# A two-layer state-space kernel on one core: layer 0's preparation for the second batch moved beside the first batch's forward scans

## The chip, the core and the metric

The kernel runs on one core of a Trainium2 chip. The metric is the device time of one execution in microseconds (us); the time of a version is the median of its runs. TensorE is called PE, VectorE DVE, ScalarE ACT, GpSimd POOL; SP is the queue that issues most DMAs. Everything is fp32.

## The reference, cut to what matters

The input x is 2 batches of 256 channels over 4096 positions. Layer 0 is a selective state-space model on the group-normed input, added to x. Layer 1 is the same model with 512 inner channels, run once forward and once with time reversed over the layer-normed result, and then eight experts of three matrix products each, mixed by a router whose features are a mean over both batches.

```python
# layer 0: group norm, then
xs, z = jnp.split(seq @ W_in, 2, axis=-1)
xc = _silu(conv_b + sum(xp[:, k:k + L, :] * conv_w[:, k] for k in range(d_conv)))
dbc = xc @ W_x
dt = softplus(dbc[..., :dt_rank] @ W_dt + b_dt)          # then Bm, Cm from dbc
h = h * exp(dt * A) + (dt * x) * B                       # per time step, 16 states
y = sum_s(h * C) + xc * D
out = (y * _silu(z)) @ W_out
# layer 1: the same with its own weights on _ln(t), forward and flipped: y_fwd + y_bwd + x
# experts on _ln(t):
feat = jnp.mean(x, axis=0); w = softmax(feat @ Wr + br)
h = relu(bn(x @ W1 + b1)); h = relu(bn(h @ W2 + b2)); y = h @ Wo + bo    # for 8 experts
out = sum_e(y[e] * w[e])
```

## The kernel before, in words

Six jobs run one after the other (`jobs`): job 0 is layer 0 of batch 0 (the first), job 1 layer 1 forward of batch 0, job 2 layer 1 backward of batch 0, and jobs 3, 4 and 5 the same of batch 1. Each job goes through 8 chunks of 512 positions. A layer-0 job has nj = 2 tiles of 128 inner channels, a layer-1 job nj = 4.

The work of a chunk is cut in quads: 32 channels by 4 states on the partitions, 4 groups of 32 channels along the free axis. Eight quads make two channel tiles. A quad has two halves, and a half is a slot, the unit of order in the whole program: 1280 slots, 16 per layer-0 chunk and 32 per layer-1 chunk. In a slot ACT makes exp(dt A) of the next slot in PSUM (`emit_decay`, L664, with the small joins L675 and the carried state L709), DVE runs one scan of 1024 steps (L690), and either DVE multiplies the states by C (L699, 760 half quads) or POOL does it for a whole or half quad (L715). POOL makes dt x times B of each quad (L654). PE sums the states into y (L723) after a first product with diag(D) (`emit_skip`, L730), whose matrix ACT builds anew for each tile of each chunk (`emit_diagonal`, L735). DVE multiplies by the gate (L742), and `finish` projects out (L761), adds x and stores.

Before its scans a chunk is prepared (`prepare`): input product xs (L414), a convolution as small matmuls (L452), its SiLU on DVE (L466, xc), the product to B, C and dt's low-rank part (L481), dt by softplus (three ACT ops, DVE L513), dt x on POOL (L517, xdt), and the gate sz (L543). dt and dt x go to DRAM and come back replicated over the states (`load_rep`, 1 MB each), B and C likewise (`load_states`). Ahead of that stands the norm: for layer 0 a scaling on ACT (L341) with group statistics, for layer 1 forward a layer norm in several steps (`norm`); backward reads back what forward stored.

The order is written out by hand. `Slots` keeps, for each slot and queue, a list of functions; `SLOTS` says at which slot before the chunk's first one each step of the preparation is issued (a product of PE in one slot, the ACT step in the next, the DVE step after that), and the main loop runs a slot's queues in the order sp, pe, sums, pe2, act, dve, pool. Each engine then works strictly in its issued order, and waits where data or a buffer isn't there. PSUM gives the preparation three banks in rotation, tanh and softplus share three buffers (`th`). The activation table is switched twice a chunk (L569), to the set with ln for the softplus and back.

`experts` plans expert work into the scan phase: from the moment a chunk's features are ready (the backward job of its batch), two halves of three layers per expert go to slots where PE (3.8 products a slot), ACT and PSUM have room by counts that every step reports (`sl.count`). They use buffers of their own: weights ew0, ew1, ew2, input en, hidden eh1 and eh2, output eu. What is finished goes to DRAM (`u_dram`). What doesn't fit by the last slot is computed in the tail, after the scans: `pairs` goes chunk by chunk and expert by expert, 24 passes of PE each (L1208, L1227), and between two of them a share of the side work of that chunk: load x, add the bias, load and add what was computed early (`add_early`, L1177 to L1179, two DVE ops each), and the router of the next chunk (`routes`). The order of chunks is by how many of their experts were computed early, fewest first. In the kernel before 81 of the 128 are early: all of batch 0's 64, and batch 1's chunks 7 and 6 with one of chunk 5.

The statistics for batch 1's group norm are made in job 2 (`chunk_stats`, L998; `group_norm`), eight loads of x with two DVE ops each.

## Time and profile before

| | us |
|---|---|
| median of 3 runs | 5111.3 |
| lowest and highest run | 5107.4, 5111.66 |
| span of the profiled execution (its only time) | 5111.0 |
| start, to the first scan | 60.0 |
| job 0, 128 slots | 466.3 |
| job 1, 256 slots | 872.5 |
| job 2, 256 slots | 882.6 |
| job 3, 128 slots | 467.5 |
| job 4, 256 slots | 876.2 |
| job 5, 256 slots | 869.9 |
| after the last scan | 616.0 |

| busy over the span | us | share |
|---|---|---|
| PE matmul | 4272.0 | 84% |
| DVE | 4580.6 | 90% |
| ACT | 3682.0 | 72% |
| POOL | 4409.1 | 86% |

The parts by job run from the start of a job's first scan to the start of the next one's. A share over the whole span hides that the parts have different limits; busy time by part is to be read with it. Idle time on an engine is charged to what ended it. A matmul's end is modelled, so a busy PE isn't PE at its peak.

### The profile page before, as it was taken

What the parts mean: (1) busy time and instruction counts of PE and PEld (TensorE: products, weight loads), DVE (VectorE), ACT (ScalarE), POOL (GpSimd) and SP (SyncE); (2) the same over time, 40 slices, a digit from 0 to 9 for tenths busy, and PEclk for the clock granted to TensorE, in tenths of its full rate; (3) what the DMA queues carried; (4) which work ended last, traced back from release to release, by engine and by line L of the source; (5) the groups of instructions that cost most, each with busy time, mean ns of one, the idle gap of its engine ahead of it and who ended that gap; (6) DMA issues with size and microseconds to landing.
All of it is one profiled execution on the core that took longest, in us unless ns stands there. A gap on an engine that the chain in (4) does not pass through costs nothing. (4 is left out here: it accounts for less than half of the span.)

```text
span 5111.0 us, 47355 instructions
## 1 busy us (share of the span) xinstructions
PE 4272.0 (84%) x14920; PEld 1474.5 (29%) x14920; DVE 4580.6 (90%) x3089; ACT 3682.0 (72%) x7476; POOL 4409.1 (86%) x1442
## 2 busy tenths in 40 slices
PE   5777767776668988988888889999999999988999
PEld 1222222221212332333322233333333333333444
DVE  6998999999999999999989999999999999936633
ACT  5777677777767888888887888888878888832232
POOL 5998999999999999999989999999999999921110
PEclk8778888888878999999999999999999999999999
DMA  5454433344444454556655545455555544555522
GB/s 179 149 176 160 165 137 125 136 136 149 156 141 155 170 177 170 187 171 201 209 182 180 181 166 200 165 179 173 181 179 181 169 166 160 175 188 181 193 103 87
DMA packets 322604, 847.85 MB, mean 166 GB/s; under 512 B 35816, under 2 KB 108016, under 8 KB 280368
## 3 DMA queue, kind: packets, MB, share of 16 engines
q1 hardware_dynamic: 318064, 817.43, 46.7%
q0 software_dynamic: 4288, 27.40, 1.4%
q8 instruction: 118, 1.93, 0.2%
q14 instruction: 134, 1.10, 0.1%
HBM read 656.88 MB, written 187.83 MB: 165 GB/s over the span
## 5 line engine op out<-in xcount | busy, mean ns | idle before, releaser
L654 POOL TENSOR_TENSOR bq<-rxdt,bc 128x2048 f32<-128x2048 f32 x640 | 2892.9, 4542 | 24.5 <-issue 13.2
L664 ACT ACTIVATE da<-rdt,w_a 128x512 f32<-128x512 f32 x2560 | 1757.0, 686 | 97.2 <-DVE bq L690 51.7
L690 DVE TENSOR_TENSOR_SCAN da<-da,h_state,bq 128x1024 f32<-128x1024 f32 x664 | 1559.1, 2348 | 44.9 <-ACT da L664 26.2
L715 POOL TENSOR_TENSOR bq<-bq,bc 128x2048 f32<-128x2048 f32 (+1 forms) x280 | 1179.8, 4214 | 22.5
L690 DVE TENSOR_TENSOR_SCAN bq<-da,h_state,bq 128x1024 f32<-128x1024 f32 x456 | 1058.6, 2338 | 20.7 <-ACT da L664 20.6
L723 PE MATMUL y<-bq,stack 128*32 128x512 f32 x5120 | 758.9, 681 | 315.1 <-POOL bq L715 294.0
L699 DVE TENSOR_TENSOR bq<-da,bc 128x1024 f32<-128x1024 f32 x760 | 926.5, 1219 | 16.0
L912 PE MATMUL e<-eh,ew 128*128 128x512 f32 x1296 | 631.1, 617 | 54.0 <-ACT eh L923 13.9
L709 ACT COPY h_state<-da 128x2 f32<-128x2 f32 x759 | 118.9, 157 | 617.7 <-DVE bq L699 615.4
L675 ACT ACTIVATE bq<-h_state,bq,a 128x1 f32<-128x1 f32 x1120 | 430.3, 384 | 0.6
L723 PEld LDWEIGHTS y<-bq,stack 128*32 128x32 f32 x5120 | 143.0, 118 | 878.6 <-POOL bq L715 416.5
L912 PEld LDWEIGHTS e<-eh,ew 128*128 128x128 f32 x1296 | 231.6, 192 | 445.4 <-issue 221.4
L1212 ACT ACTIVATE h<-hp,of,sc 128x512 f32<-128x512 f32 x188 | 145.9, 777 | 290.8 <-PE hp L1208 272.7
L452 PE MATMUL conv<-xs,w_conv 64*64 64x512 f32 x2560 | 332.1, 608 | 21.7 <-ACT xs L436 17.8
L414 PE MATMUL z<-nx,w_in 128*128 128x512 f32 x640 | 324.9, 639 | 26.5 <-DVE sp L513 12.0
L414 PE MATMUL xs<-nx,w_in 128*128 128x512 f32 x640 | 316.6, 624 | 23.4 <-DVE xc L466 8.4
L912 PE MATMUL e<-en,ew 128*128 128x512 f32 x648 | 308.4, 605 | 28.3 <-DVE fcen L809 15.7
L761 PE MATMUL o<-sz,w_out 128*128 128x512 f32 x640 | 306.3, 619 | 0.0
L923 ACT ACTIVATE eh<-e,of,sc 128x512 f32<-128x512 f32 x324 | 245.6, 769 | 30.6 <-PE e L912 30.2
L517 POOL TENSOR_TENSOR xdt<-sp,xc 128x512 f32<-128x512 f32 x160 | 203.4, 1275 | 49.7 <-DVE sp L513 49.7
L730 PE MATMUL y<-xc,w_d 128*128 128x512 f32 x320 | 193.5, 689 | 56.5 <-DVE sz L742 56.3
L690 DVE TENSOR_TENSOR_SCAN da<-da,bq 128x1024 f32<-128x1024 f32 x96 | 219.5, 2287 | 5.3 <-issue 2.5
(139 smaller groups left out, 4914.3 us busy)
## 6 DMA issues: line engine op xcount, KB each, us to landing
rxdt<-xdtd SPq DMA_DIRECT2D x160, 1024.0 KB, 6.8
rdt<-dtd SPq DMA_DIRECT2D x160, 1024.0 KB, 6.6
bc<-bcd SPq DMA_DIRECT2D x384, 256.0 KB, 3.3
ew<-in_W SPq DMA_DIRECT2D x162, 256.0 KB, 4.4
u<-u SPq DMA_DIRECT2D x81, 512.0 KB, 4.3
dtd<-sp SPq DMA_DIRECT2D x160, 256.0 KB, 3.5
xdtd<-xdt SPq DMA_DIRECT2D x160, 256.0 KB, 3.8
u<-eu SPq DMA_DIRECT2D x77, 512.0 KB, 6.7
```

What stands on the lines that cost most here:

```text
L414: nc.tensor.matmul(ps, job.w["in", half][:, k, j * P : (j + 1) * P], rhs, start=(k == 0), stop=(k == KC - 1),)
L452: nc.tensor.matmul(v[r][64 * col : 64 * col + 64, :], job.w["conv"][rows, 2 * jp + j, k, :], ck["xs", jp][rows, j, k : k + T] if k < 4 els ...
L654: nc.gpsimd.tensor_tensor(bq[g], ck["rxdt", j], over_groups(ck["bc", 0, sg]), ALU.mult)
L664: nc.scalar.activation(da[g, h][:, k, :], cks[i]["rdt", j][:, q, :], AF.Exp, scale=steps[i][0].w["a"][:, j, q * SG + sg : q * SG + sg + 1],)
L675: nc.scalar.activation(bq[g][:, q, 0:1], job.h[:, j, sg, q : q + 1], AF.Identity, scale=cks[i]["a0", j][:, h, sg : sg + 1], bias=bq[g][:, ...
L690: nc.vector.tensor_tensor_scan(b if on_pool(g, h) else d, d, b, job.h[:, j, sg, 2 * h : 2 * h + 1] if c else 0.0, ALU.mult, ALU.add,)
L699: nc.vector.tensor_tensor(bq[g][:, two, :], d, cks[i]["bc", 1, sg].rearrange("p (o t) -> p o t", o=1).to_broadcast([P, 2, T]), ALU.mult,)
L715: nc.gpsimd.tensor_tensor(b, b, cks[i]["bc", 1, sg].rearrange("p (o t) -> p o t", o=1).to_broadcast([P, groups, T]), ALU.mult,)
L723: nc.tensor.matmul(y[i, j][q * CG : (q + 1) * CG, :], stack, bq[g][:, q, :], start=False, stop=(sg == SG - 1),)
L761: nc.tensor.matmul(v[m], job.w["out"][:, j, m * P : (m + 1) * P], ck["sz", j], start=False, stop=(j == job.nj - 1),)
L912: nc.tensor.matmul(ps, ew[l][:, k, m * P : (m + 1) * P], key[x][:, k, :], start=(k == 0), stop=(k == KC - 1),)
L923: nc.scalar.activation(key[dst][:, m, :], key["ps", l, m], AF.Relu, bias=of[:, l, e, m : m + 1], scale=sc[:, l, e, m : m + 1],)
```

## The change

The preparation of job 3 (layer 0 of batch 1) no longer stands before each of its chunks. Chunk c of it is issued within the slots of chunk c + 1 of job 1 (for c = 7, the first chunk of job 2), at the slots of `AHEAD_SLOTS` from that chunk's first one. Its input x and its xc take turns in eh1, the scaled input is in en, sz in eu; xc, sz, dt, dt x and B, C go to DRAM tensors of their own, and job 3 loads xc and sz back tile by tile (16 loads each). The counts for the planner go to the slots where the steps now are.

Layer 0's large weights (W_in, convolution, W_x, W_dt) are loaded once, in the experts' buffers ew0, ew1, eh2 and ew2, and serve both layer-0 jobs; layer 1's keep their own. W_dt is loaded into both halves of the partitions, since job 3's B, C, dt rows take partitions 64 to 127 of the tile that job 1 uses.

Batch 1's statistics move to job 0 (a load every 14 slots, in eu), its group norm to 11 slots before job 1. Around it, job 1's own steps move by one or a few slots (`late`, `xs`, `log`), and the ln table is chosen earlier there, so that both softplus run under one choice. Job 3 switches no tables of its own.

D's diagonals are built once a job, in one buffer for all its tiles, two slots before the tile's first use (slot 8j - 2). The averaging matrix of the layer norms is a column read with a zero step; the group norm's matrix is rebuilt at each of its two uses.

In the built program this makes 86 early experts instead of 81 (batch 1's chunk 5 has six, not one), 20 diagonals instead of 160, 98 table loads instead of 116, and 1862 entries in SP's order instead of 1793.

```diff
+AHEAD = 3
+AHEAD_SLOTS = dict(x=-7, scale=-5, xs=(-1, 0), conv=(2,), dbc=10, dt=(14, 22), z=(-4, 12))
+NARROW_W = {"w_in0": "ew0", "w_in1": "ew1", "w_conv": "eh2"}
...
-    mean_w = const.tile([P, P], F32, name="mean_w")
-    nc.vector.memset(mean_w, 1.0 / C)
...
+    columns = const.tile([P, 6], F32, name="columns")
+    one_col, eps3, eps5, eps10, huge, mean_col = (columns[:, k : k + 1] for k in range(6))
+    for column, value in (
+        (one_col, 1.0), (eps3, 1e-3), (eps5, 1e-5), (eps10, 1e-10), (huge, HUGE), (mean_col, 1.0 / C),
+    ):
         nc.vector.memset(column, value)
+    mean_w = mean_col.to_broadcast([P, P])
...
+        dbc_rows = const.tile([P, T], F32, name="dbc_rows")
...
         def load_weights(job, tag, s0):
             nj, w = job.nj, {}
             job.w = w
+            job.matrices = jobs[0].w if job is jobs[AHEAD] else w
+
+            def weight(key, home, shape, name):
+                if job.layer:
+                    w[key] = wp.tile(shape, F32, tag=home, name=f"{name}_{tag}")
+                elif key == "dt":
+                    w[key] = w["x_dt"][:, nj * XC : nj * XC + shape[1]]
+                elif key == "x":
+                    w["x_dt"] = wk.tile([P, KC * C], F32, tag="ew2", name=f"{name}_{tag}")
+                    w[key] = w["x_dt"][:, : nj * XC].rearrange("p (j n) -> p j n", j=nj)
+                else:
+                    w[key] = wk.tile(shape, F32, tag=NARROW_W[home], name=f"{name}_{tag}")
...
-                nc.sync.dma_start(w["dt"], job.params["W_dt"])
+                weight("dt", "w_dt", [XC, job.din], "w_dt")
+                for rows in range(0, P if job.layer == 0 else XC, XC):
+                    nc.sync.dma_start(w["dt"][rows : rows + XC, :], job.params["W_dt"])
...
+            def halve():
                 nc.scalar.mul(w["conv"][:, :, 4, :], w["conv"][:, :, 4, :], 0.5)
...
+            def diagonal(j):
+                if j == 0:
+                    job.diagonal = wp.tile([P, nj, P], F32, tag="w_d", name=f"w_d_{tag}")
+                nc.scalar.mul(
+                    job.diagonal[:, j, :].rearrange("p (q c) -> p q c", q=SG),
+                    ident.rearrange("p (c q) -> p q c", q=SG), w["vec"][:, j, V_D : V_D + 1],
+                )
+
+            for j in range(nj):
+                sl.put(s0 + 8 * j - 2, "act", lambda j=j: diagonal(j))
             sl.put(s0 - 39, "sp", load_small)
+            sl.put(s0 - 31, "act", small)
+            sl.put(s0 + 19, "sp", load_out)
+            if job is jobs[AHEAD]:
+                return
...
-            sl.put(s0 - 31, "act", small)
+            sl.put(s0 - 31, "act", halve)
...
+            if job is not jobs[AHEAD]:
+                keep(job, "kept", tag)
...
+            g16 = wk.tile([P, T], F32, tag="th", name=f"g16_{tag}", bufs=3)
+            g16, blk8 = g16[:, : P // 8], g16[:, P : 2 * P]
+            nc.vector.tensor_reduce(g16, ident.rearrange("p (g k) -> p g k", k=8), AX.X, ALU.add)
+            nc.vector.tensor_scalar(
+                blk8.rearrange("p (g k) -> p g k", k=8),
+                g16.rearrange("p (g o) -> p g o", o=1).to_broadcast([P, P // 8, 8]),
+                1.0 / 8, None, ALU.mult,
+            )
...
+            if job is jobs[AHEAD]:
+                return
...
+            late = 1 if NCH < i < 2 * NCH else 0
             for d, queue, fn in (
                 (-48, "sp", load_x), (-44, "pe", mean), (-43, "dve", centre), (-42, "act", square),
-                (-41, "pe", variance), (-40, "act", roots), (-39, "dve", divide), (-39, "pool", add),
+                (late - 41, "pe", variance), (late - 40, "act", roots), (late - 39, "dve", divide), (late - 39, "pool", add),
                 (-35 if c else -38, "act", affine), (-34, "sp", store),
...
+            if NCH < i <= 2 * NCH + 1:
+                at = dict(at, xs=(-31, -29, -24, -23), log=-18)
+            ahead = job is jobs[AHEAD]
+            at_rows = slice(XC, 2 * XC) if ahead else slice(0, XC)
+
+            def of_chunk(key, j, bufs, home):
+                if not ahead:
+                    ck[key, j] = wk.tile([P, T], F32, tag=key, name=f"{key}_{tag}_{j}", bufs=bufs)
+                else:
+                    if j == 0:
+                        ck[key] = wk.tile([P, KC, T], F32, tag=home, name=f"{key}_{tag}")
+                    ck[key, j] = ck[key][:, j, :]
+                return ck[key, j]
+
+            def stored(key):
+                ck[key, "d"] = drp.tile([P, KC, T], F32, name=f"{key}d_{tag}")
+                nc.sync.dma_start(ck[key, "d"], ck[key])
+
+            def loaded(key, j, bufs):
+                ck[key, j] = wk.tile([P, T], F32, tag=key, name=f"{key}_{tag}_{j}", bufs=bufs)
+                nc.sync.dma_start(ck[key, j], ck[key, "d"][:, j, :])
+
+            def scaled():
+                ck["nx"] = wk.tile([P, KC, T], F32, tag="en", name=f"nx_{tag}")
+                for k in range(KC):
+                    nc.scalar.activation(
+                        ck["nx"][:, k, :], ck["x"][:, k, :], AF.Identity,
+                        bias=job.gb[:, k : k + 1], scale=job.gs[:, k : k + 1],
+                    )
...
+            def load_x():
+                ck["x"] = wk.tile([P, KC, T], F32, tag="eh1", name=f"x_{tag}")
+                nc.sync.dma_start(
+                    ck["x"], a["x"][job.batch].rearrange("(k p) l -> p k l", p=P)[:, :, job.cols(c)]
+                )
...
-                    ck["xc", j] = wk.tile([P, T], F32, tag="xc", name=f"xc_{tag}_{j}", bufs=6)
                     nc.vector.scalar_tensor_tensor(
-                        ck["xc", j], th[r], 1.0, v[r], ALU.add, ALU.mult
+                        of_chunk("xc", j, 6, "eh1"), th[r], 1.0, v[r], ALU.add, ALU.mult
...
-                    ck["dbc"] = wk.tile([XC, T], F32, tag="dbc", name=f"dbc_{tag}")
-                    nc.scalar.activation(ck["dbc"], v["ps"][:XC], AF.Identity, bias=one_row[:XC])
-                    ck["bc"] = bcd.tile([2, NS, T], F32, tag="bc", name=f"bcd_{tag}")
+                    ck["dbc"] = dbc_rows[at_rows, :]
+                    nc.scalar.activation(ck["dbc"], v["ps"][at_rows, :], AF.Identity, bias=one_row[at_rows])
+                    ck["bc"] = (
+                        drp.tile([2, NS, T], F32, name=f"bcd_{tag}") if ahead
+                        else bcd.tile([2, NS, T], F32, tag="bc", name=f"bcd_{tag}")
+                    )
...
-                        v["ps"], job.w["dt"][:, j * P : (j + 1) * P], ck["dbc"], start=True, stop=True
+                        v["ps"], job.matrices["dt"][at_rows, j * P : (j + 1) * P], ck["dbc"], start=True, stop=True
...
                 def store(key):
-                    d = ck["rep", key, j] = bcd.tile(
-                        [P, T], F32, tag=f"{key}{j}", name=f"{key}d_{tag}_{j}"
+                    d = ck["rep", key, j] = (
+                        drp.tile([P, T], F32, name=f"{key}d_{tag}_{j}") if ahead
+                        else bcd.tile([P, T], F32, tag=f"{key}{j}", name=f"{key}d_{tag}_{j}")
...
-                    ck["sz", j] = wk.tile([P, T], F32, tag="sz", name=f"sz_{tag}_{j}", bufs=8)
                     nc.vector.scalar_tensor_tensor(
-                        ck["sz", j], v["th"], 1.0, v["ps"], ALU.add, ALU.mult
+                        of_chunk("sz", j, 8, "eu"), v["th"], 1.0, v["ps"], ALU.add, ALU.mult
...
-                sl.put(s0 + at["xs"][0], "act", lambda: start_job(job, tag))
+                sl.put(s0 + SLOTS[nj]["xs"][0], "act", lambda: start_job(job, tag))
+            if ahead:
+                for j in range(nj):
+                    sl.put(s0 + 8 * j - 10, "sp", lambda j=j: loaded("xc", j, 6))
+                    sl.put(s0 + 8 * j - 4, "sp", lambda j=j: loaded("sz", j, 8))
+                at, s0 = AHEAD_SLOTS, starts[NCH + 1 + c]
+                if c == 0:
+                    sl.put(s0 + at["xs"][0], "act", lambda: keep(job, "kept_ahead", tag))
+                put(at["x"], [(0, "sp", load_x), (at["scale"] - at["x"], "act", scaled)])
+                put(at["conv"][0] + 5, [(0, "sp", lambda: stored("xc"))])
+                put(at["z"][-1] + 4, [(0, "sp", lambda: stored("sz"))])
...
-            for slot, table in ((at["dt"][0], "natural_log_exp_and_others"), (at["z"][0], "exp_and_others")):
+            for slot, table in () if ahead else ((at.get("log", at["dt"][0]), "natural_log_exp_and_others"), (at["z"][0], "exp_and_others")):
...
-            nc.tensor.matmul(y[i, j], diag.pop((i, j)), cks[i]["xc", j], start=True, stop=False)
-
-        def emit_diagonal(i, j):
-
-            d = diag[i, j] = wk.tile([P, P], F32, tag="w_d", name=f"w_d_{tags[i]}_{j}", bufs=2)
-            nc.scalar.mul(
-                d.rearrange("p (q c) -> p q c", q=SG), ident.rearrange("p (c q) -> p q c", q=SG),
-                steps[i][0].w["vec"][:, j, V_D : V_D + 1],
+            nc.tensor.matmul(
+                y[i, j], steps[i][0].diagonal[:, j, :], cks[i]["xc", j], start=True, stop=False
...
             def load():
-                v["x"] = wk.tile([P, KC, T], F32, tag="x", name=f"xst_{n}")
+                v["x"] = wk.tile([P, KC, T], F32, tag="eu", name=f"xst_{n}")
                 nc.sync.dma_start(
...
         for n in range(NCH):
-            chunk_stats(n, starts[2 * NCH + n // 2] + 16 * (n % 2))
-        sl.put(starts[2 * NCH + 5], "dve", lambda: group_norm(st6, jobs[len(jobs) // NB], "1"))
+            chunk_stats(n, 14 * n + 3)
+        sl.put(starts[NCH] - 11, "dve", lambda: group_norm(st6, jobs[AHEAD], "1"))
...
-                if (n, h) in ((0, 0), (4, 0)):
-                    emit_diagonal(i, 2 * jp + n // SG)
```

## The prediction

> **What bounds the kernel now.** I read the busy table, then asked for it again stretch by stretch. The cuts are the starts of the first scan (L690) of each job: 1280 scans stand in a fixed order, 128 in each layer-0 job, 256 in each layer-1 job. A slot is one scan. In the answer each row is a stretch, its length, then busy time of PE, PEld, DVE, ACT and POOL with instruction counts, the granted clock, DMA share and GB/s; before the first row come 60.0 us of start.
>
> ```profile
> core 0: us, PE busy (x) PEld busy (x) DVE busy (x) ACT busy (x) POOL busy (x), PEclk, DMA share, GB/s
> 60.00:526.30 466.30, 326.98 (x1164) 103.03 (x1164) 433.46 (x282) 347.57 (x716) 441.95 (x142) 0.80 0.49 168
> 526.30:1398.80 872.50, 607.67 (x2310) 181.47 (x2312) 855.08 (x556) 635.57 (x1341) 867.99 (x278) 0.82 0.40 139
> 1398.80:2281.40 882.60, 748.12 (x2762) 249.81 (x2759) 860.82 (x572) 690.60 (x1430) 865.30 (x273) 0.93 0.49 169
> 2281.40:2748.90 467.50, 406.82 (x1450) 135.60 (x1449) 430.71 (x282) 391.49 (x786) 431.56 (x140) 0.96 0.57 195
> 2748.90:3625.10 876.20, 787.06 (x2890) 271.56 (x2889) 857.08 (x556) 721.17 (x1486) 869.99 (x278) 0.96 0.52 177
> 3625.10:4495.00 869.90, 793.83 (x2841) 272.58 (x2840) 844.78 (x539) 698.19 (x1434) 847.55 (x269) 0.97 0.51 170
> 4495.00:5111.00 616.00, 571.01 (x1390) 248.27 (x1389) 281.03 (x268) 173.76 (x236) 76.81 (x58) 0.97 0.43 151
> ```
>
> Six rows are jobs 0 to 5, the last is the expert tail. In the layer-1 jobs DVE (97 to 98%) and POOL (97 to 99.5%) bind together. In the layer-0 jobs, first and fourth row, each has some 36 us free: there it is latency of chained small steps as well. In the tail PE binds (93%). So work taken off ACT or PE during scans is worth little; work moved between jobs is worth what DVE and POOL do with it; work taken out of the tail is worth PE time. The groups of instructions give the durations (busy, mean ns, idle before):
>
> ```profile
> L517 POOL TENSOR_TENSOR xdt<-sp,xc 128x512 f32<-128x512 f32 x160 | 203.4, 1275 | 49.7 <-DVE sp L513 49.7
> L466 DVE SCALAR_TENSOR_TENSOR xc<-thx,conv 128x512 f32<-128x512 f32 x160 | 108.4, 679 | 41.6 <-ACT thx L461 41.4
> L513 DVE SCALAR_TENSOR_TENSOR sp<-dt,sp 128x512 f32<-128x512 f32 x160 | 107.7, 673 | 20.8 <-ACT h_state L709 13.7 <-ACT sp L510 6.7 <-issue 0.4
> L543 DVE SCALAR_TENSOR_TENSOR sz<-thz,z 128x512 f32<-128x512 f32 x160 | 107.1, 670 | 2.4 <-ACT thz L539 2.4
> L569 ACT ACT_TABLE_LOAD x96 | 123.2, 1283 | 1.7
> L735 ACT ACTIVATE w_d<-ident,vec 128x128 f32<-128x128 f32 x160 | 82.2, 514 | 0.0
> ```
>
> The tail I read in the timeline, first PE, then DVE (start, length, instruction):
>
> ```profile
> 5074.37 3.60 PE L1208 MATMUL hp<-n,W 128*128 128x512 f32 x8
> 5077.80 3.87 PE L1208 MATMUL hp<-h,W 128*128 128x512 f32 x8
> 5081.51 3.60 PE L1227 MATMUL y<-h,Wo 128*128 128x512 f32 x8
> 5084.94 3.60 PE L1208 MATMUL hp<-n,W 128*128 128x512 f32 x8
> ```
>
> ```profile
> 5060.47 1.23 DVE L1178 TENSOR_TENSOR u<-u,wb 128x1024 f32<-128x1024 f32 x1 [5.84 <-DMA u<-u]
> 5061.73 1.23 DVE L1179 TENSOR_TENSOR x<-x,u 128x1024 f32<-128x1024 f32 x1
> 5062.88 1.22 DVE L1178 TENSOR_TENSOR u<-u,wb 128x1024 f32<-128x1024 f32 x1
> ```
>
> An expert of one chunk takes PE 5084.94 - 5074.37 = 10.57 us; adding one computed earlier takes DVE 5062.88 - 5060.47 = 2.41 us.
>
> **What the Trainium skill says.** "PSUM — Partial Sum Buffer", section "Engine vs sequencer instructions": the queues of ScalarE, VectorE and GpSimd are strict FIFO. So one late operand holds everything behind it; the trace agrees (ACT's copy L709 stood 615.4 us in 490 waits for DVE, all of ACT behind it). "SBUF — State Buffer", section "SBUF: two separate sides": a DVE op with two SBUF inputs and a GpSimd op exclude each other. The prep ops read one operand in PSUM and run at 0.67 us beside a POOL that is 99.5% busy, so moving them pays no such lock; in the tail one x+u beside a POOL add took 3.35 us instead of 1.23, which agrees. "ScalarE: Activation LUTs", section "What ACT_TABLE_LOAD costs": 1283 ns, as the row above.
>
> **The change, part by part.**
>
> Job 3's prep is, per chunk: on DVE two xc, two sp, two sz, 2 x (0.679+0.673+0.670) = 4.05 us; on POOL two xdt, 2.55 us; on ACT about 10 us and two table loads, 2.57 us; on PE 15 matmul units (one is two passes of 0.43 us, 0.86; eight passes follow one another in 3.43 us in the tail's timeline). Now chunk c of it runs inside chunk c+1 of job 1 (the last in job 2's first).
>
> 1) *Job 1.* Seven of its chunks take one each. DVE pays 7 x 4.05 = 28; POOL 7 x 2.55 = 18. Job 1 has 17.4 us of DVE idle and 4.5 of POOL idle in 872.5, so the floor is between 868+18 = 886 (+14) and 872.5+28 = 901 (+28). ACT rises to about 0.78 and PE to 0.81 of the stage, shares that jobs 2, 4 and 5 bear without DVE losing.
> Friction comes on top, for each queue the moved steps pass. SP gets per chunk an x load, stores of xc, sz and B/C, two of dt and two of xdt: eight more to about 45 in 110 us. The x load is the bad one: its buffer, eh1, then holds xc, last read by POOL's second xdt at slot 24, and the load stands at slot 25. In this job an xdt ends 6 to 11 us after its slot's scan starts (row starts of L517 against those of L690), and this one stands behind one more 4.5 us product. So the load leaves some 9.5 to 13 us after slot 24 begins and lands about 4.5 later (512 KB from x: 4.1 median for xr, 6.3 for x), at slot 28 to 29 of 3.4 us each. ACT's scaling, which waits for it, stands at slot 27; behind it are the carry and the decay exponentials of slot 29, and DVE waits for those. Loss: from 0 (POOL less late) to 3.8 us a chunk; I take 1. A th buffer (three, now taken also by two sp and four tanh more) and PSUM banks reused with a slot's margin: 0.5 to 1. Together 1.7 x 7 = 12. Job 1: +40 (from +18 to +58).
> 2) *Job 0.* Batch 1's statistics come here: 16 bn_stats, 10.1 us in the trace, and the group norm, which in its old place held DVE 6.2 us (ops 2.3, waits for PE 1.7 and ACT 2.3), plus 0.5 to rebuild the averaging matrix. Some 33 us of DVE idle are here; I let half of the statistics vanish in them: +11 (0 to +17).
> 3) *Job 2.* Loses that work, -16; gains the last piece of moved prep, +4, loses the first chunk's own, -4; its last half chunk, 58.6 us where like ones take 55.5, eases: -18 in all.
> 4) *Job 3.* DVE loses 7 x 4.05 = 28, POOL 18, ACT about 99 (16 table loads in it). POOL's floor is 431.6-18 = 414, DVE's 402. PE stays level: the planner puts 119 half layers of experts here instead of 63, by its own slots in the built kernel, and 98 + 238 units stand for 208 + 126. By halves of chunks (16 slots), those without prep last 50.9 to 52.1 us elsewhere (ends of jobs 5 and 2): 5 x 51.5 = 257.5. The last three, with job 4's first preparation, lasted 184.7; less 6 of prep and some 9 of waits on a fuller ACT: 170. Sum 428, -39 (-20 to -47). The loads of xc and sz (32 more) and of rdt, rxdt have their data in DRAM long before; cover: slots -10 and -4 against first use at +4 and later.
> 5) *D's diagonals.* 160 - 20 = 140 x 0.514 = 72 us off ACT. It is hidden by DVE and POOL everywhere: -3 in jobs 4 and 5; a lighter PE in the first 64 slots of job 5 (1 expert half layer for 37) another -2. The single buffer makes each job's first diagonal, two slots before the job, wait for the last skip matmul four slots before: nothing unless PE is over 6 us late. mean_w as a stepless column: the trace shows such an operand only as the moving one (one_col, 589 ns, no slower); if weight loads doubled, about 250 x 0.19 = 48 us of PE, mostly under DVE; taken as nothing. Early weight loads: within the -39.
> 6) *Tail.* The built kernel has 86 experts early instead of 81, so 42 are left instead of 47: 5 x 10.57 = -53. But all five are of the chunk worked on last, which now has two pairs left instead of seven, and the side work (x load, bias, 8 + 6 adds) stands between these two on DVE. From the start of the last but one pair: before, PE alone, 5111.0 - 5074.4 = 37 us. After: x+u can start when the bias is in, 15; seven adds 33; weigh, eighth add 37; SP's store of that chunk stands ahead of the next u loads, +5.4 to land, 43; six adds 58; weigh, last layer, final add, store 67. That gives back 30: -23 (-53 if hidden after all, -15).
>
> Before the first scan nothing changes that waits: other buffers, the same loads, 60 us. Sum on the profiled 5111.0 us, which is its span (median of the runs 5111.3): +40+11-18-39-5-23 = -34. **5077 us.**
>
> **Rivals.**
> *Job 1 turns it round* (slower): the x load behind POOL's xdt. Every us of it counts seven times. With 1 a chunk I forecast 5077; from 1 + (5121-5077)/7 = 7.3 a chunk it is slower. For: POOL there is 99.5% busy and already 11 us late. Against: my reading gives at most 3.8, and a delayed DVE lets POOL catch up. With all other waits growing too, 9 a chunk: 5133.
> *The tail pays in full*: the adds hide or PE sets the end, 5077-30 = 5047. For: DVE is 46% busy there; against: all side work is in the last two pairs.
> *Job 3 does not shrink*: latency, not DVE, spaces it, and PE, (336 x 0.86 + 82 of sums and skips)/428 = 0.87 by passes and 0.95 as the profile counts busy, becomes its bound: -7 instead of -39, 5109, no difference. For: its DVE was only 92% busy; against: rows without prep elsewhere.
>
> **How the numbers follow.** The forecast 0.5 (own range 5058 to 5096), tail in full 0.16, job 3 unshrunk 0.16, job 1 turns it round 0.12, the rest 0.06. A difference under 0.2% (10 us) can't be told from none here. Range 5040 to 5115: below it a tail in full with a lucky job 1, above it the slow rival. Faster 0.75, same 0.13, slower 0.12.
>
> **What would show it.** By the same cuts: job 0 477, job 1 912, job 2 865, job 3 428, jobs 4 and 5 1741, tail 593. In job 1, ACT's wait before the scaling (L341 before) for the DMA of x, some us a chunk; in the tail's end DVE adds back to back and PE idle some 25 us. I am wrong if job 3 stays above 450, if job 1 passes 935, or if L690's idle for ACT grows in job 0.

## The result and the profile after

The changed kernel takes 5073.0 us (median of 4 runs, 5071.1 to 5080.4) against 5110.1 for the kernel before beside it: a ratio of 0.9928, with a 95% interval of 0.9916 to 0.9940. It is faster by 37 us, where 34 were forecast (5077). Its profiled execution has a span of 5070.5 us, 40.5 less than before.

The busy table of the kernel after, by the same cuts (each row: stretch, its length, busy us and instructions of PE, PEld, DVE, ACT and POOL, granted clock, DMA share, GB/s):

```profile
core 0: us, PE busy (x) PEld busy (x) DVE busy (x) ACT busy (x) POOL busy (x), PEclk, DMA share, GB/s
61.60:531.30 469.70, 325.30 (x1168) 101.36 (x1168) 444.74 (x306) 343.03 (x704) 442.76 (x142) 0.82 0.51 174
531.30:1428.30 897.00, 695.84 (x2767) 216.22 (x2768) 877.93 (x601) 687.93 (x1435) 888.34 (x293) 0.89 0.46 159
1428.30:2299.70 871.40, 751.87 (x2751) 254.79 (x2749) 846.87 (x546) 674.51 (x1388) 861.40 (x272) 0.94 0.49 168
2299.70:2730.40 430.70, 392.07 (x1278) 143.78 (x1276) 407.04 (x242) 345.90 (x704) 413.21 (x126) 0.97 0.68 235
2730.40:3608.90 878.50, 786.46 (x2872) 271.87 (x2872) 855.76 (x557) 708.13 (x1454) 870.51 (x278) 0.95 0.52 176
3608.90:4477.60 868.70, 740.34 (x2697) 250.00 (x2696) 842.81 (x540) 666.60 (x1369) 846.34 (x269) 0.94 0.46 160
4477.60:5070.50 592.90, 524.77 (x1274) 228.62 (x1272) 288.50 (x272) 159.01 (x217) 78.10 (x59) 0.94 0.46 163
```

| us | before | after | difference | forecast |
|---|---|---|---|---|
| start | 60.0 | 61.6 | +1.6 | 0 |
| job 0 | 466.3 | 469.7 | +3.4 | +11 |
| job 1 | 872.5 | 897.0 | +24.5 | +40 |
| job 2 | 882.6 | 871.4 | -11.2 | -18 |
| job 3 | 467.5 | 430.7 | -36.8 | -39 |
| jobs 4 and 5 | 1746.1 | 1747.2 | +1.1 | -5 |
| tail | 616.0 | 593.0 | -23.0 | -23 |
| sum | 5111.0 | 5070.5 | -40.5 | -34 |

Every sign but that of jobs 4 and 5 came as forecast. In job 1 (second row) DVE's busy time rose from 855.1 to 877.9 us and POOL's from 868.0 to 888.3, and the stretch by about as much: the moved work sits on the two engines that bind there. In job 3 (fourth row) DVE's share rose from 92.1% to 94.5% although it lost 24 us of work (430.7 to 407.0). In the tail PE's share fell from 92.7% to 88.5%: PE has 46 us of work less, and the stretch is only 23 us shorter.

The groups of instructions after, with the lines that answer to those shown before (xdt, xc, sp and sz, the table loads of the softplus, D's diagonals; columns as there):

```profile
L590 POOL TENSOR_TENSOR xdt<-sp,xc 128x512 f32<-128x512 f32 x160 | 203.3, 1275 | 46.0 <-DVE sp L586 45.8
L536 DVE SCALAR_TENSOR_TENSOR xc<-thx,conv 128x512 f32<-128x512 f32 x160 | 108.5, 679 | 35.3 <-ACT thx L532 33.7 <-ACT h_state L792 1.2
L586 DVE SCALAR_TENSOR_TENSOR sp<-dt,sp 128x512 f32<-128x512 f32 x160 | 107.6, 672 | 20.5 <-ACT h_state L792 12.3 <-ACT sp L583 6.7 <-ACT bq L758 1.6
L616 DVE SCALAR_TENSOR_TENSOR sz<-thz,z 128x512 f32<-128x512 f32 x160 | 107.2, 670 | 2.4 <-ACT thz L613 2.4
L652 ACT ACT_TABLE_LOAD x80 | 102.6, 1283 | 1.4
L275 ACT ACTIVATE w_d<-ident,vec 128x128 f32<-128x128 f32 x20 | 10.3, 513 | 0.0
```

All counts of the preparation are the old ones, at the old durations: of these steps nothing is done less often but the table loads and the diagonals. The moved steps are not cheaper, they are placed elsewhere.

The end of the tail, PE's timeline of the kernel after (the first line is where the last but one pair starts; a pair is one expert's work on one chunk):

```profile
5000.46 3.60 PE L1283 MATMUL hp<-n,W 128*128 128x512 f32 x8
...
5013.04 3.70 PE L1283 MATMUL hp<-n,W 128*128 128x512 f32 x8
5016.58 3.88 PE L1283 MATMUL hp<-h,W 128*128 128x512 f32 x8
5020.29 7.03 PE L1302 MATMUL y<-h,Wo 128*128 128x512 f32 x16
5035.11 6.23 PE L1302 MATMUL y<-h,Wo 128*128 128x512 f32 x8 [7.79 <-DVE h L1294]
5059.01 6.23 PE L1302 MATMUL y<-h,Wo 128*128 128x512 f32 x8 [17.67 <-DVE h L1294]
```

PE is done with its hidden layers at 5020 and then waits twice, 7.79 and 17.67 us, for DVE to weigh a pair (L1294), that is, to multiply its hidden layer by the router's weight. After each wait eight passes take 6.23 us where eight take 3.60 in the first line. DVE's timeline there:

```profile
5036.22 1.22 DVE L1254 TENSOR_TENSOR x<-x,u 128x1024 f32<-128x1024 f32 x1
5043.30 1.23 DVE L1253 TENSOR_TENSOR u<-u,wb 128x1024 f32<-128x1024 f32 x1 [5.85 <-DMA u<-u]
...
5057.74 1.22 DVE L1294 TENSOR_TENSOR h<-h,wb 128x1024 f32<-128x1024 f32 x1
5058.88 1.22 DVE L1307 TENSOR_TENSOR x<-y,x 128x1024 f32<-128x1024 f32 x1
5065.28 1.22 DVE L1307 TENSOR_TENSOR x<-y,x 128x1024 f32<-128x1024 f32 x1 [5.19 <-PE y L1302]
```

The last chunk of positions has all eight experts of batch 0 and six of batch 1 to add. Batch 0's eight adds end at 5037.4; the loads of batch 1's parts stand in SP's queue behind batch 0's store, and the first add that needs one starts at 5043.3; six adds of 2.4 us follow one another, and only then is the last pair weighed.

### The profile page after: what moved, and what is told of

It reads as the page before. It is cut to its first block, busy times and chain, and to the rows that moved or that the text cites. A ratio compares the mean times of both kernels' runs of the same rounds, so it can differ in the third digit from the quotient of the medians.

```text
span 5070.5 us, 47370 instructions
## 1 busy us (share of the span) xinstructions
PE 4247.6 (84%) x14920; PEld 1478.8 (29%) x14920; DVE 4581.4 (90%) x3096; ACT 3609.1 (71%) x7319; POOL 4409.8 (87%) x1442
## 5 line engine op out<-in xcount | busy, mean ns | idle before, releaser
L747 ACT ACTIVATE da<-rdt,w_a 128x512 f32<-128x512 f32 x2560 | 1757.3, 686 | 110.3 <-DVE bq L773 63.9
L806 PE MATMUL y<-bq,stack 128*32 128x512 f32 x5120 | 741.9, 665 | 275.3 <-POOL bq L798 251.5
L989 PE MATMUL e<-eh,ew 128*128 128x512 f32 x1376 | 671.6, 622 | 63.9 <-DMA ew<-in_Wo 17.0
L989 PEld LDWEIGHTS e<-eh,ew 128*128 128x128 f32 x1376 | 250.7, 194 | 475.9 <-issue 239.9
L989 PE MATMUL e<-en,ew 128*128 128x512 f32 x688 | 323.8, 604 | 22.9 <-DVE fcen L886 15.8
L1287 ACT ACTIVATE h<-hp,of,sc 128x512 f32<-128x512 f32 x168 | 130.4, 777 | 252.2 <-PE hp L1283 235.6
L1000 ACT ACTIVATE eh<-e,of,sc 128x512 f32<-128x512 f32 x344 | 259.3, 767 | 44.1 <-PE e L989 43.9
L1248 POOL TENSOR_TENSOR x<-x,bi 128x1024 f32<-128x1024 f32 x16 | 37.2, 2338 | 188.8 <-DMA x<-t_dram 108.0
```

The source lines that it names most:

```text
L747: nc.scalar.activation(da[g, h][:, k, :], cks[i]["rdt", j][:, q, :], AF.Exp, scale=steps[i][0].w["a"][:, j, q * SG + sg : q * SG + sg + 1],)
L806: nc.tensor.matmul(y[i, j][q * CG : (q + 1) * CG, :], stack, bq[g][:, q, :], start=False, stop=(sg == SG - 1),)
L989: nc.tensor.matmul(ps, ew[l][:, k, m * P : (m + 1) * P], key[x][:, k, :], start=(k == 0), stop=(k == KC - 1),)
L1000: nc.scalar.activation(key[dst][:, m, :], key["ps", l, m], AF.Relu, bias=of[:, l, e, m : m + 1], scale=sc[:, l, e, m : m + 1],)
```

## The experiments

The theory: the time of each stretch is set by DVE and POOL in the scans and by PE in the tail, and the moved preparation costs its DVE and POOL time plus one wait for x a chunk. Against it stand: that the denser expert plan, which the freed slots of job 3 bring, is where time went or came from; that the diagonals matter; that the tail's loss has another cause.

| us | median | ratio to before | 95% interval |
|---|---|---|---|
| the change | 5073.0 | 0.9928 | 0.9916 to 0.9940 |
| the old plan of experts | 5077.4 | 0.9933 | 0.9917 to 0.9948 |
| five early experts fewer | 5074.4 | 0.9929 | 0.9915 to 0.9942 |
| x in a buffer of its own | 5069.3 | 0.9921 | 0.9907 to 0.9934 |
| a diagonal for every tile again | 5079.3 | 0.9938 | 0.9926 to 0.9951 |
| before, with the statistics in job 0 | 5108.4 | 0.9994 | 0.9986 to 1.0002 |
| before, with the column for mean_w | 5112.0 | 0.9999 | 0.9991 to 1.0008 |
| the short chunk last but one in the tail | 5057.7 | 0.9896 | 0.9883 to 0.9910 |
| both remedies | 5056.8 | 0.9893 | 0.9879 to 0.9906 |
| both, routing after each add | 5066.5 | 0.9904 | 0.9888 to 0.9921 |
| both, routing two chunks ahead | 5046.7 | 0.9871 | 0.9855 to 0.9888 |

The ratio is the one on record; it can differ from the quotient of the medians by up to 0.001.

The stretches of their profiled executions, by the same cuts:

| us | start | job 0 | job 1 | job 2 | job 3 | job 4 | job 5 | tail |
|---|---|---|---|---|---|---|---|---|
| before | 60.0 | 466.3 | 872.5 | 882.6 | 467.5 | 876.2 | 869.9 | 616.0 |
| the change | 61.6 | 469.7 | 897.0 | 871.4 | 430.7 | 878.5 | 868.7 | 593.0 |
| the old plan of experts | 60.2 | 470.3 | 896.8 | 863.9 | 425.3 | 877.7 | 866.6 | 616.1 |
| five early experts fewer | 63.1 | 468.5 | 897.7 | 873.6 | 431.4 | 877.4 | 860.4 | 603.0 |
| x in a buffer of its own | 63.1 | 468.4 | 890.8 | 874.3 | 430.5 | 878.4 | 868.4 | 593.1 |
| a diagonal for every tile again | 62.8 | 470.2 | 897.6 | 873.9 | 429.0 | 876.8 | 870.8 | 593.1 |
| before, statistics in job 0 | 59.7 | 472.3 | 871.3 | 875.1 | 466.3 | 876.4 | 869.9 | 615.3 |
| before, column for mean_w | 60.5 | 463.2 | 872.4 | 883.3 | 466.4 | 876.4 | 869.7 | 613.3 |
| short chunk last but one | 60.6 | 469.8 | 896.9 | 871.8 | 430.0 | 879.1 | 870.4 | 582.8 |
| both remedies | 60.5 | 469.3 | 890.9 | 873.9 | 430.7 | 878.5 | 868.5 | 581.1 |
| both, routing after each add | 60.0 | 470.2 | 890.9 | 873.9 | 434.0 | 878.7 | 868.6 | 591.4 |
| both, routing two chunks ahead | 61.4 | 467.8 | 891.0 | 871.5 | 433.6 | 877.9 | 868.3 | 574.5 |

Where a kernel has a line more than another, the numbers of the lines after it are higher by one (L1198 is the change's L1197). Stretches in which two kernels have the same instructions in the same order differ by up to some 4 us from one profiled execution to the next (the start, job 2, job 3 in the rows above), so a single difference under that is not read.

**The old plan of experts.** The moved steps report their counts to the planner at the slots where they stood before; everything else is as in the change.

```diff
+            cs0, cat = s0, at
...
-                sl.count(s0 + at["xs"][j], 2, 1, (1,))
+                sl.count(cs0 + cat["xs"][j], 2, 1, (1,))
...
-            sl.count(s0 + at["dbc"], nj, 1, (1,))
+            sl.count(cs0 + cat["dbc"], nj, 1, (1,))
```

> The moved preparation alone: everything as changed, but the planner is told the old slots for job 3's steps, so it makes the old plan: 81 early experts, 63 expert half layers in job 3 instead of 119. Theory A (job 3 is held by DVE and POOL, PE's denser experts cost it nothing): job 3 stays at 431 +- 3, the tail goes back to 616, total 5073 + 23 = 5096. Theory B (the denser experts hold job 3 too: in the changed kernel's trace DVE there loses 4.8 us at once behind an expert whose weights landed late): job 3 falls to 423 or less, total 5088 or less.

Measured: 5077.4 us. With the plan of before (81 early experts, 63 half layers of them in job 3) all of the change but the fuller plan is worth 34 us of the profiled execution (5111.0 to 5076.9). Its rows of the busy table for jobs 2 and 3 and the tail:

```profile
1427.30:2291.20 863.90, 727.66 (x2693) 243.65 (x2692) 846.21 (x545) 667.21 (x1376) 854.60 (x271) 0.94 0.48 166
2291.20:2716.50 425.30, 330.25 (x1058) 108.86 (x1057) 405.70 (x242) 311.66 (x647) 419.28 (x127) 0.88 0.61 208
...
4460.80:5076.90 616.10, 573.56 (x1390) 249.55 (x1388) 282.71 (x268) 174.01 (x236) 77.84 (x58) 0.96 0.43 151
```

So the fuller plan is not free in the scans. It costs 7.5 us in job 2 (871.4 against 863.9; all kernels with the fuller plan have 871.4 to 874.3) and 5.4 in job 3 (430.7 against 425.3; 429.0 to 434.0), for 23.1 in the tail. The old plan has one profile, so the 5.4 is little more than the scatter. With the start (+1.4) and differences of some 2 us or less in the rest, 6.4 us remain of it in the profiled execution, 4.4 in the medians, which the intervals don't tell from none. Job 3 carries 62 us more PE work (392.1 against 330.3) in 5.4 us more time. One stall stands out in the timeline of the change (start, length, instruction, idle before and what ended it):

```profile
2509.51 3.75 PE L989 MATMUL e<-eh,ew 128*128 128x512 f32 x4 [5.30 <-DMA ew<-in_Wo]
...
2513.30 0.59 ACT L998 COPY eu<-e 128x512 f32<-128x512 f32 x1 [4.25 <-PE e L989]
...
2519.88 2.35 DVE L773 TENSOR_TENSOR_SCAN bq<-da,h_state,bq 128x1024 f32<-128x1024 f32 x1 [4.79 <-ACT da L747]
```

An expert's weights land late, PE begins its last layer 5.30 us late, ACT's copy of the result waits 4.25 us for PE, the decay exponentials (L747) stand behind that copy, and DVE's scan waits 4.79 us for them. The queue of ACT is a strict FIFO by the Trainium skill ("PSUM — Partial Sum Buffer", section "Engine vs sequencer instructions"), and here, too, the exponentials start only after the copy: at this place a late expert becomes a late scan.

This stall does not account for job 3's 5.4 us, though. Over the whole of job 3 DVE waits 13.6 us for L747 in the change and 12.4 for the same exponentials with the old plan. By half chunks (16 slots), the first five, in which the stall lies, cost 1.0 us more than with the old plan (258.6 against 257.6) and the last three 4.4 (172.1 against 167.7). What makes the difference there is not shown.

In job 2 the place is plain: up to its last 16 slots the two plans agree to within 1.3 us, and these take 59.5 us with 53.2 of PE in the change, 50.7 with 37.5 of PE here. DVE's waits in these slots of the change:

```profile
DVE da L773 <- ACT da L747: 4.9, 3, 2.8
DVE bq L773 <- ACT da L747: 3.2, 3, 1.5
```

With the old plan the trace shows no wait of DVE in these slots. So 8.1 of the 8.8 us are scans that wait for ACT. ACT has 43.7 us of work in these slots against 38.2, and waits 3.3 for products of the experts; which of the two makes it late was not separated.

**Five early experts fewer.** The plan of the change, its last five experts left to the tail.

```diff
-            emit_experts(put)
+            emit_experts(put[:81])
```

> As changed, but the last five early experts are left to the tail (81 early, as before). By the forecast's tail step (five experts save 53 us of PE and the adds give back 30): tail 616, total 5073 + 23 = 5096. If the five also cost the scans something, jobs 5 and its end get shorter and the total is 5090 or less. If the tail had saved the full 53, 5126.

Measured: 5074.4 us, no difference from the change that can be told. I had expected the tail to return to that of before; it rose by 10 us only, to 603.0, and job 5 fell by 8.3. Its rows for job 5 and the tail:

```profile
3611.70:4472.10 860.40, 710.69 (x2616) 234.47 (x2612) 842.23 (x539) 654.27 (x1349) 844.73 (x267) 0.92 0.45 156
4472.10:5075.10 603.00, 558.59 (x1352) 242.17 (x1352) 280.76 (x267) 167.68 (x227) 75.98 (x56) 0.96 0.43 152
```

The 47 experts left are as many as with the old plan, but PE is busy 15 us less after the last scan than there (558.6 against 573.6): there the plan runs on past the last scan and the tail starts behind it. So the five experts taken early at the end of job 5 bought nothing that can be told: they cost 8.3 us of scans and shortened the tail by 10.

**x in a buffer of its own.** The x of the moved preparation goes to eu, where it takes turns with sz, and no longer with xc in eh1; "its own" means no more than that.

```diff
-                ck["x"] = wk.tile([P, KC, T], F32, tag="eh1", name=f"x_{tag}")
+                ck["x"] = wk.tile([P, KC, T], F32, tag="eu", name=f"x_{tag}")
```

> As changed, but the moved preparation's x goes to eu instead of eh1, so that its load no longer waits for POOL's last product with xc. The x wait theory: ACT's seven waits for x in job 1 (12.1 us in the changed kernel's trace) go, job 1 falls by 4 to 8 us from 897, total 5067. The rival, that DVE and POOL are the floor of job 1 and swallow the waits: job 1 within 2 us of 897, total unchanged.

In the change, the waits of ACT, of SP's queue and of DVE in job 1 (us in total, times, longest) name the chain:

```profile
ACT nx L485 <- DMA x<-in_x: 12.1, 7, 3.4
```

```profile
SPq L492 <- POOL xdt L590: 33.0, 7, 4.8
```

```profile
DVE da L773 <- ACT da L747: 12.1, 10, 2.8
```

SP waits 33.0 us in seven times for POOL's xdt, which reads the xc in the same buffer; ACT's scaling then waits 12.1 us for the x. With x in eu the first of these lines is gone from job 1, SP waits there for no xdt at L492 (its waits for xdt at the stores of dt and xdt, L597, rise from 10.9 to 36.7 us), and DVE's line reads

```profile
DVE da L773 <- ACT da L747: 6.3, 7, 0.9
```

and job 1 takes 890.8 us instead of 897.0 (890.8 to 891.0 in the four kernels with x in eu, 896.8 to 897.7 in the five others with the moved preparation). The wait cost 6.2 us, 0.9 a chunk. The busy row of job 1 with x in eu:

```profile
531.50:1422.30 890.80, 692.60 (x2761) 219.34 (x2762) 877.51 (x600) 687.82 (x1435) 885.48 (x292) 0.89 0.46 159
```

What is left of job 1's rise, 18.3 us, goes with POOL's: it is busy 17.5 us more than before and idle 5.3 us, as before (4.5), while DVE's idle time fell from 17.4 to 13.3. That POOL and not DVE sets it is read from these two, not tested by taking work off one of them.

**A diagonal for every tile again.** The change with D's diagonals built per tile, as before.

```diff
-            for j in range(nj):
-                sl.put(s0 + 8 * j - 2, "act", lambda j=j: diagonal(j))
...
+                if (n, h) in ((0, 0), (4, 0)):
+                    emit_diagonal(i, 2 * jp + n // SG)
```

> As changed, but D's diagonals are built for each tile of each chunk again (160 instead of 20 ACT operations of 0.51 us). The forecast (hidden under DVE and POOL): +3 us, not to be told from none. The rival, that ACT is on the path of the scans: 0.2 to 0.5 us for each of the 140, +30 to +70.

Measured: 5079.3 us, its interval overlapping that of the change (0.9926 to 0.9951 against 0.9916 to 0.9940). ACT has its 72 us of diagonals back:

```profile
L818 ACT ACTIVATE w_d<-ident,vec 128x128 f32<-128x128 f32 x160 | 82.1, 513 | 0.0
```

No stretch of the scans moved by more than 2.5 us, in both directions; the span is 3.8 us longer, of which 1.2 lie before the first scan. Building them once is worth between nothing and 6 us; most of the 72 us is hidden in the scans.

**Before, with the statistics in job 0.** One part of the change alone, on the kernel before.

```diff
-                v["x"] = wk.tile([P, KC, T], F32, tag="x", name=f"xst_{n}")
+                v["x"] = wk.tile([P, KC, T], F32, tag="eu", name=f"xst_{n}")
...
-            chunk_stats(n, starts[2 * NCH + n // 2] + 16 * (n % 2))
-        sl.put(starts[2 * NCH + 5], "dve", lambda: group_norm(st6, jobs[len(jobs) // NB], "1"))
+            chunk_stats(n, 14 * n + 3)
+        sl.put(starts[NCH] - 11, "dve", lambda: group_norm(st6, jobs[len(jobs) // NB], "1"))
```

> The kernel before with one part of the change alone: batch 1's statistics and its group norm in job 0 instead of job 2. From the changed kernel's trace: job 0 +3, job 2 -11, total -8 on 5110, 5102. The forecast's sizes: job 0 +11, job 2 -16, total 5105. If the statistics had nothing to do with job 2's gain there: job 2 unchanged, 5113.

Job 0 rises by 6.0, job 2 falls by 7.5, the time doesn't change beyond its interval. DVE's busy time in job 0 rose by 11.4 us (433.5 to 444.9), so half of it went into idle time that was there anyway. In job 2 DVE lost 11.3 us of work (860.8 to 849.6), and two thirds of that came back as time.

**Before, with the column for mean_w.** The averaging matrix as one column read with a zero step, on the kernel before.

```diff
-    mean_w = const.tile([P, P], F32, name="mean_w")
-    nc.vector.memset(mean_w, 1.0 / C)
...
+    mean_w = mean_col.to_broadcast([P, P])
```

> The kernel before with one part of the change alone: the averaging matrix of the layer norms is one column read with a zero step. The forecast: nothing, 5110 +- 5. If a weight load with a zero step were twice as long: some 48 us more on PE, weight loads of the mean and variance products at 0.4 us instead of 0.2, and a few us of time.

No difference, and the groups of weight loads say why. Before:

```profile
L354 PEld LDWEIGHTS mean<-x,mean_w 128*128 128x128 f32 x64 | 13.2, 208 | 22.6 <-issue 16.1 <-DVE sp L513 6.1 <-ACT bq L675 0.5
L788 PEld LDWEIGHTS fmean<-xr,mean_w 128*128 128x128 f32 x60 | 11.4, 190 | 14.4 <-issue 11.2 <-ACT da L664 2.6 <-ACT bq L675 0.2
```

with the column:

```profile
L353 PEld LDWEIGHTS mean<-x,columns 128*128 128x128 f32 x64 | 13.2, 208 | 22.6 <-issue 16.1 <-DVE sp L512 6.1 <-ACT bq L674 0.5
L787 PEld LDWEIGHTS fmean<-xr,columns 128*128 128x128 f32 x60 | 11.4, 190 | 14.3 <-issue 11.2 <-ACT da L663 2.6 <-ACT bq L674 0.2
```

208 and 190 ns a load either way: a weight operand with a zero step loads as fast as a stored matrix.

**The short chunk last but one in the tail.** In the change the chunk with two experts left is worked on last. Here it changes places with the one before it, so that eight pairs of PE work end the program.

```diff
         rest.sort(key=lambda i: sum(first[b, i] for b in range(NB)))
+        rest.insert(-1, rest.pop())
```

> As changed, but in the tail the chunk with two experts left goes last but one, and a chunk with eight left goes last. The add theory (the end is set by 14 adds of early experts on DVE between the last two pairs, 30 us given back): tail 593 falls by 20 to 30, total 5043 to 5053. The rival, that another thing sets the end of the tail (PE or the stores): within 5 us of 5073.

Measured: 5057.7 us; the tail is 582.8 us, 10.2 less and not the 20 to 30 that full recovery would give. PE's waits in this tail (us, times, longest) tell where the rest went. Two of them in the change:

```profile
PE wt L1222 <- DVE w L1216: 3.3, 2, 1.7
PE var_m L1183 <- ACT sq L1180: 2.4, 1, 2.4
```

and here:

```profile
PE lt L1198 <- POOL nm L1191: 15.5, 2, 12.4
PE wt L1223 <- DVE w L1217: 13.8, 3, 10.5
PE hp L1284 <- DMA n<-nf_dram: 12.6, 1, 12.6
PE var_m L1184 <- ACT sq L1181: 6.8, 1, 6.8
```

The two waits at the end (7.79 and 17.67) are gone, 25.5 us. But the two pairs of the short chunk now stand in front of another chunk, whose router steps are issued beside the fourteen adds: its softmax (L1217, DVE) comes behind adds, and PE's transposes wait 10.5 us longer for it; its variance waits 6.8 where it was 2.4. 25.5 - 10.5 - 4.4 = 10.6, close to the gain seen, 10.2. Part of the stall had gone from the end to the routing of the last chunk.

**Both remedies.** x in eu and the short chunk last but one.

> As changed, with x in eu and the chunk with two experts left last but one. If both work and add up: 5073 - 6 - 25 = 5042. If the tail order alone works: 5048.

Measured: 5056.8 us, 9 us above even the figure for the tail order alone, which had the tail's gain too large. Job 1 and the tail each show their own gain (890.9 and 581.1); the gains lie in different stretches and add up in the profiled execution, 5053.4. In the medians that doesn't show: 5056.8 against 5057.7 for the order of chunks alone.

**Both, routing after each add.** Of the next chunk's router steps, one is issued after each add instead of after every third, so that the softmax comes ahead of most adds.

```diff
-            every = max(1, len(now) // max(1, len(ahead)))
+            every = 1
```

> Both remedies (x in a buffer of its own, the chunk with two experts left worked on last but one), and within the next chunk's routing steps put one after each add instead of one after every third. Theory: with the two-left chunk moved, the end of the tail is TensorE without a break, but 15 of the 25 us so regained were lost again before it, because the routing of the last chunk (variance 4.4 us more, transposed weights 10.5) stands behind adds on VectorE. With the routing ahead of the adds the tail falls from 581 to 571 us (568 to 575) and the median from 5056.8 to about 5047. Rival: VectorE and the loads of the adds hold this part whatever their order, and the wait only moves to another instruction: tail 578 to 583, median 5054 to 5059.

Measured: 5066.5 us, the wrong way, by neither theory's figure. The waits aimed at are gone, the one for variance back to 2.4 us and that for the softmax to 1.7 at most, but another took their place (PE's waits in the tail):

```profile
PE lt L1198 <- POOL nm L1191: 36.8, 3, 14.0
```

The steps of a router depend on one another: variance, the scaled n, POOL's sum over the batches (L1191), PE's logits. Issued closer together, PE comes to the logits before POOL's sum is there. So being early is not enough for them; here they needed room between them, too.

**Both, routing two chunks ahead.** The spacing of the change, but the last chunk is routed in the eight pairs of the chunk third from the end, not in the two pairs that carry the adds; its weights get a third buffer.

```diff
+            if at == len(rest) - 3:
+                after = rest[at + 1 :]
+            elif at == len(rest) - 2:
+                after = []
             for j in whole[at : at + 1] + after:
                 ahead += routes(j)
...
-            wb[i] = mk.tile([P, E, T], F32, tag="wb", name=f"wb_{i}")
+            wb[i] = mk.tile([P, E, T], F32, tag="wb", name=f"wb_{i}", bufs=3)
```

> Both remedies (x in a buffer of its own, the chunk with two experts left worked on last but one), the adds and routing steps spaced as in the changed kernel, but the routing of the last chunk is given to the eight pairs of the chunk third from the end, beside the routing of the next one, so that none is left for the two pairs that carry the fourteen adds; its weights get a third buffer. Theory: the steps of a chunk's routing need a pair of TensorE work between them (the logits wait for GpSimd's sum otherwise, 36.8 us where they were put after every add) and must not stand behind adds: with both, TensorE's waits for the variance and the transposed weights (6.8 and 13.3 us with both remedies alone) fall below 6 together and those for the sum stay under 22: tail 566 to 574 us, median 5042 to 5050. Rival: the waits move on to another instruction again: tail 579 or more, median 5055 or more.

Measured: 5046.7 us, 0.9871 of before (0.9855 to 0.9888), in the forecast range. PE's waits in its tail:

```profile
PE lt L1198 <- POOL nm L1191: 14.4, 2, 11.8
PE hp L1284 <- DMA n<-nf_dram: 12.6, 1, 12.6
PE wt L1223 <- DVE w L1217: 5.0, 3, 1.7
PE y L1303 <- DVE h L1295: 4.2, 1, 4.2
PE var_m L1184 <- ACT sq L1181: 2.4, 1, 2.4
```

The tail is 574.5 us, a hair above the 566 to 574 named for it. The waits for softmax and variance sum to 7.4 us, not under 6, but the longest is 1.7 and 2.4; of what is left, 24.4 us are two waits, for the first n and for one chunk's logits, that stood in the tail before the change too (13.5 and 12.0 there), and 4.2 are one pair that is weighed behind adds. This is the best version found, 26 us below the change.

## Why the prediction was right, and which steps were not

The forecast, 5077, missed the median by 4 us, but not every step was that good: jobs 0 and 1 came out 23 us below their forecasts, and the start, jobs 2 to 5 and the tail together some 17 above. The errors partly cancel, and that is luck.

*Job 1, +40, measured +24.5.* The mechanism was right, two terms were mis-sized. I took the upper end of the floor, +28: all of DVE's new work on top of the old stretch, with none of it in the 17.4 us that DVE was idle. (DVE's floor proper is 855 + 28 = 883, below POOL's 886.) With the x wait taken away the rise is 18.3 us, close to POOL's 17.5. DVE's own rise was 22.8 us rather than 28, since an operation in a row of others costs less than its duration. DVE's timeline in job 1 of the change:

```profile
640.17 0.66 DVE L616 SCALAR_TENSOR_TENSOR sz<-thz,z 128x512 f32<-128x512 f32 x1
640.75 2.34 DVE L773 TENSOR_TENSOR_SCAN bq<-da,h_state,bq 128x1024 f32<-128x1024 f32 x1
```

The next scan starts 0.58 us after an operation of 0.66. With x in its own buffer DVE is idle 13.3 us against 17.4 before: 4 us of its work vanished there. Friction was put at 1.7 us a chunk, 12: the x wait, put at 1 a chunk, measured 0.9 (6.2 in all); the rest, buffers and banks reused with a slot's margin, put at 0.5 to 1, is not to be found.

*Job 0, +11, measured +3.4*, and 6.0 with the statistics moved alone. The step "I let half of the statistics vanish" was too careful: DVE's busy time rose by 11.3 us in the change, and two thirds of it met idle time. The group norm had been charged in full, with 4.0 us of waits; in job 0 its waits for PE and ACT are 1.9. The idle time was the right sort of cover, taken too small. The scans' idle for ACT, which I had named as a sign of being wrong if it grew, went from 9.5 to 10.7 us: no new wait of weight.

*Job 2, -18, measured -11.2.* Two terms failed. The statistics were put at -16; moved alone they took 11.3 us off DVE and 7.5 off job 2. And "its last half chunk, 58.6 us where like ones take 55.5, eases" did not hold: it took 59.5, since the fuller plan also puts more experts into the end of job 2. With the old plan it took 50.7, 7.9 less than before, so that the -18.7 of the whole job there, so near the forecast, is made of other terms and is luck.

*Job 3, -39, measured -36.8.* Right, and the rows by half chunks too: the first five last 258.6 us (257.5 forecast), the last three 172.1 (170). But the 119 half layers were costed at nothing, with PE level, and with the old plan job 3 is 5.4 us shorter, -42.2; the gain of the preparation was underestimated by about as much. The rival that job 3 doesn't shrink is out: the stretch follows the lighter work of DVE and POOL even with PE at 91%.

*Diagonals, mean_w, jobs 4 and 5, -5, measured +1.1.* Hidden, as said; but the 3 us that the diagonals and the 2 that a lighter PE in job 5 were to give are not there. With five early experts fewer job 5 is 860.4, 9.5 below before, so the five at its end may have taken back what a lighter PE gave. In jobs 4 and 5 the kernel with a diagonal for every tile takes 1747.6 us, the change 1747.2. The single buffer's wait at a job's first diagonal cost nothing that shows.

*Tail, -23, measured -23.0.* The working stood, its terms to some 3 us. From the start of the last but one pair to the end it is 70 us (5000.46 to 5070.5) where 67 were forecast, so 33 were given back and not 30, and the rest of the tail fell by some 3 more than the 53 of five experts. PE waits 25.5 us at the end (some 25 forecast) behind adds of 2.4 us, and the store stands ahead of the loads; the slower passes after the waits (6.23 instead of 3.60, twice) add 5.3. Changing the chunks' places removed just these waits.

Of the rivals, the tail did not pay in full; even with the short chunk and the routing moved it is 574.5 us, where -53 would make it 563. Job 1 did not turn it round, at 0.9 us a chunk where 7.3 would have decided.

Open: in job 2 the fuller plan costs time because the scans of its last 16 slots wait for ACT, but what makes ACT late was not separated; in job 3 the cause of its 5.4 us is not shown, since DVE's waits for the exponentials are 1.2 us longer only. The experts of job 3 placed more thinly were run only as the whole old plan. The 16 table loads that fell away were not taken apart from the moved preparation, and the diagonals once a job were not run on the kernel before.

## What to carry to other kernels

When work moves under other work, price it by the engine that has least idle time in the place it goes to (here POOL's 17.5 us, not DVE's 28), and look in the waits for who last read the buffer that its first load goes into. A planner that fills the freed slots is a second change with its own bill, and keeping its counts while moving the work shows that bill apart. A chunk with little work left has no cover for its side work: put it where other work follows, and give the next chunk's chain of small steps a place that is neither behind that side work nor too close together.

## What the runs showed of the hardware that was not expected

- Small DVE operations in a row overlap at their ends in the trace: 0.66 us long, 0.58 from start to start; with 45 more instructions in job 1 DVE was busy 22.8 us longer, 0.51 each.
- A weight load whose operand is one column read with a zero step took 208 and 190 ns, as with the stored matrix.
- After waits of 7.79 and 17.67 us at the end of the tail PE took 6.23 us for eight passes, where eight took 3.60 just before.
- 46 us of PE work less in the tail went with 23 us less time there; 62 us more in job 3, to 91% of the stretch, went with 5.4 us more.
- A 512 KB load of x took 3.6 to 7.2 us from issue to landing, 4.7 in the median; in SP's queue it had stood up to 4.8 us behind its own wait before that.
